# A lightning-attention kernel: second value weights loaded two units sooner, splits in halves, token normalisation on ScalarE, and other orders in the plain units and the first tile

## The chip, the cores and the metric

The kernel runs on one core of one Trainium2 chip. The metric is the device time in microseconds (us), the median of three runs. A core has five engines that work side by side, each with its own queue of instructions in order: TensorE (PE; its weight loads are listed as PEld) multiplies matrices into the accumulator memory PSUM, VectorE (DVE), ScalarE (ACT) and GpSimd (POOL) do elementwise work, and SyncE (SP) issues the transfers (DMAs) between the chip's main memory and the on-chip memory SBUF. ACT can issue DMAs too. An engine waits for another through semaphores; an instruction that waits holds up all that stand behind it in its queue.

## The reference

x has 4 sequences of 512 tokens with 512 features. Each token is normalised over its features (layer norm). Three things are computed from the normalised xn:

- q, k and v are silu of linear projections of xn, for 16 heads of 128. Within a sequence, blocks of tokens are taken in order, with a state that decays by a slope of the head:

```python
o_inter = einsum(qi * q_decay, kv)
o_intra = einsum(einsum(qi, ki) * diag_decay, vi)
kv_new  = block_decay * kv + einsum(ki * k_decay, vi)
```

- the heads' outputs are divided by their root mean square over all 2048 values, weighted, multiplied by sigmoid of another projection of xn (the gate), and projected back to 512 features: s.
- a router takes a softmax over 64 logits of xn, keeps the 8 largest weights, and forms xn times their sum plus a mix of 64 bias rows; silu of that is g.

The output is x + s * g. All inputs are 32-bit floats.

## The kernel before

**Products.** Each large product runs in a 32-bit matmul type on operands split in two: hi is the rounded value (`split_hi`, L99, always on ACT) and lo the rest (`split_lo`, L102, a subtraction on DVE or POOL). Three of the four hi/lo combinations are multiplied. Each projection is taken as a 2x2 by 2x2 block product. `unit` (L469) does it with seven products in place of eight (`PRODUCTS`, L39): the weights give A11, A12, A22 and four sums S1 to S4 (`sum_of`, L409), the tokens give B11, B21, B22 and four combinations T1 to T4 (`token_sums`, L261). A product is six matmuls of 128x512. Partial results are added on DVE from PSUM (L478), so a unit needs three PSUM banks, of four that there are. `plain_unit` (L510) does the eight plain products with A11, A12, A21, A22 and needs no sums.

**v's stage.** It comes first and is the one that the change touches. The 16 heads' v weights come in two halves, `ws[0]` and `ws[1]`; the tokens in two pairs of sequences p and four tiles t of 128 tokens a sequence. With `k` counting units, units 0 to 7 take all eight tile pairs with the first half, units 8 to 15 with the second (L900). Units 0 and 1 are plain ones, since the sums S are not ready then. A unit's silu is a sigmoid on ACT (`silu_of`, L536) and a product on DVE that is deferred (`do_deferred`) to a later point of the order.

**Tokens.** For each tile pair, `prepare` (L796) gives a list of steps: "stats" (`layer_norms`: mean and variance on DVE, and the reciprocal root on POOL by a power, L233), "norms" (`normalise_x`: one DVE operation a sequence, L205), "turn" (transposes on PE and copies to SBUF on ACT, and a store of the result), "sums" and "more" (combinations and splits of the token blocks, on POOL from the second tile on) and "logits" (router matmuls, L308). Unit k hosts the turn, sums, more and logits of tile k + 1, and stats and norms of tile k + 2, and issues the loads of tile k + 3.

**Order.** It is written out by hand. `after[i]` holds the steps that are issued after product i of a unit (`unit`), or after a pair of products in a plain unit (L526). All engines' queues follow this program order. Buffers are pools with a fixed count: the raw v weights have one buffer, the split v weights eight (tag "w"), x tiles four.

**Weights.** The first half's loads are interleaved with the first x loads (L859 to L864), its splits are spread over the start and units 0 and 1. The second half's eight loads of 256 KB are issued in unit 4 (L923), its sums in units 4 to 7 (two on DVE, two on POOL), its splits from unit 6 to unit 8 (L929).

**Start.** Slopes, the router weight and bias and norm_w are loaded from ACT's queue. ACT computes the decay tables `mkdecay` (16 activations of 128x256, exp) in two lots, four before the first split and 12 after the second tile's stats. POOL masks them, and 16 stores write them to main memory. `warm_up` runs transposes with no use of the result.

The stages after v's (gate, q and k projections and attention by heads, then the output projection) are the same in both kernels.

Of the kernel before, what the change touches and what calls it, by code (L numbers as in the profile page):

```python
# [50 lines left out]
def kernel(  # L51
# [13 lines left out]
    nc = tc.nc  # L65
# [5 lines left out]
    NT = N // P  # L71
# [18 lines left out]
    small = pool(ctx, "small", 4)  # L90
# [8 lines left out]
    def split_hi(hi, src):  # L99
        nc.scalar.copy(hi, src)  # L100
# [5 lines left out]
    slopes = const.tile([P, NH], F32, tag="slopes", name="slopes")  # L106
# [97 lines left out]
    def normalise(dst, src, b, t):  # L204
        nc.vector.tensor_scalar(  # L205
            dst, src, stats[b][:, t, 0:1], rstd[b][:, t : t + 1], ALU.subtract, ALU.mult
        )
# [8 lines left out]
    xts = {}  # L216
# [3 lines left out]
        nc.sync.dma_start(out=xt, in_=x[tok(b, t), :])  # L220
        xts[b, t] = xt

    def layer_norms(p, t):
        var = small.tile([P, PB], F32, tag="lnvar", name=f"lnv_{p}_{t}")
        for j in range(PB):
            b = p * PB + j
            st = small.tile([P, nc.vector.BN_STATS_DIM], F32, tag="bn", name=f"bn_{b}_{t}")
            nc.vector.bn_stats(st, xts[b, t])
            nc.vector.bn_aggr(stats[b][:, t, :], st)
            nc.vector.tensor_scalar(  # L230
                var[:, j : j + 1], stats[b][:, t, 1:2], 1.0, LN_EPS, ALU.mult, ALU.add
            )
        nc.gpsimd.tensor_tensor(rstd_of[p][:, t], var, mhalf[:, 0:PB], ALU.pow)  # L233

    def normalise_x(bs, t):
        for b in bs:
            normalise(xts[b, t], xts[b, t], b, t)

    xfs = {}

# [149 lines left out]
    class Weights:  # L390
# [37 lines left out]
        def place(self, n):  # L428
            self.of[n] = self.wp.tile([P, 2, self.width], F32R, tag="w", name=f"w_{n}_{self.name}")

        def split_one(self, n, eng):
            src = self.sum[int(n[1]) - 1] if n[0] == "S" else self.raw[:, int(n[1]) - 1, int(n[2]) - 1]
            if n not in self.of:
                self.place(n)
            split_hi(self.of[n][:, 0], src)

            m = 2 if eng is nc.gpsimd else 1
            for i in range(m):
                c = bass.ts(i, self.width // m)
                split_lo(eng, self.of[n][:, 1, c], src[:, c], self.of[n][:, 0, c])  # L440

        def splits(self, lo_engines):
# [67 lines left out]
    def plain_unit(name, operands, sink, after):  # L510
        for i in range(2):
            ps = [ps_mm.tile([P, N], F32, tag="mm", name=f"d{i}{j}_{name}") for j in range(2)]
            for k in range(2):
                for j in range(2):
                    xn = (("B11", "T1"), ("B21", "B22"))[k][j]
                    for c in range(KC):
                        for n, (wi, xi) in enumerate(PASSES):
                            lhsT, rhs = operands(f"A{i + 1}{k + 1}", xn, wi, xi, c)
                            nc.tensor.matmul(
                                ps[j], lhsT, rhs, start=(k == 0 and c == 0 and n == 0),  # L520
                                stop=(k == 1 and c == KC - 1 and n == len(PASSES) - 1),
                            )
                    if k == 1:
                        do_deferred()
                        sink(i, j, ps[j])
                for fs in after[3 * i + k :][: 1 if k == 0 else 2 + i]:  # L526
                    for f in fs:
                        f()

# [16 lines left out]
    def do_deferred(keep=0):  # L546
        while len(deferred) > keep:
            deferred.pop(0)()
# [245 lines left out]
    NP_FIRST = 2  # L794

    def prepare(stage, p, t):  # L796
        bs = [p * PB + j for j in range(PB)]

        def turn():
            for j in range(PB):  # L800
                transpose(stage, p, j, t)
            if p == 0:
                nc.sync.dma_start(out=xf_d[t], in_=xfs[p, t])

        if p == 0 and t < NP_FIRST:
            sums = (lambda: plain(p, t, nc.vector if t == 0 else nc.gpsimd)), lambda: None
        else:
            sums = combine(stage, p, t, nc.gpsimd)

        def route_logits():  # L810
            logits(stage, p, t)
        return {
            "stats": lambda: layer_norms(p, t), "norms": lambda: normalise_x(bs, t),
            "turn": turn, "sums": sums[0], "more": sums[1], "logits": route_logits,
        }

# [36 lines left out]
    ws = [v_weights(0, g, rawp, sump, vwp) for g in range(NV)]  # L853
# [2 lines left out]
    n1 = len(tiles)  # L856
    prep = [prepare(stage, p, t) for p, t in tiles]

    nc.scalar.dma_start(out=slopes, in_=slope.to_broadcast([P, NH]))  # L859
    load_pair(stage, 0, 0)  # L860
    vloads = ws[0].load()
    vloads(4)
    load_pair(stage, 0, 1)
    vloads(4)  # L864
    nc.scalar.dma_start(out=rw, in_=router_w)
    nc.scalar.dma_start(out=rb, in_=router_b.to_broadcast([P, E]))
    nc.scalar.dma_start(out=nw, in_=norm_w)
    make_first()
    make_dist()
    warm_up(WARM)  # L870
    for i, n in enumerate(XN):
# [8 lines left out]
    ds[0] = make_decays(ds[0], hs[0])  # L880
    prep[0]["stats"]()
    prep[0]["norms"]()
    ws[0].split_one("A11", nc.vector)
    prep[0]["turn"]()
    load_pair(stage, *tiles[2])
    mask_decays(ds[0], hs[0])
    warm_up(6)
    prep[0]["sums"]()
    ws[0].split_one("A12", nc.gpsimd)
    prep[0]["logits"]()  # L890
    prep[1]["stats"]()
    prep[1]["norms"]()
# [7 lines left out]
    for k, (p, t) in enumerate(tiles + again):  # L900
        g, after = k // n1, nothing()
        for unit_of, what in ((n1 - 3, (0, "top")), (n1 - 2, (0, "less")), (n1 + 2, (1, "top")), (n1 + 3, (1, "less"))):
            if k == unit_of:
                after[2].append(lambda what=what: scores_less(*what))
        if n1 - NT <= k < n1:
            after[6].append(lambda p=p, t=t: keep_blocks(p, t))
        if k + 1 < n1:
            after[0].append(prep[k + 1]["turn"])
            if k + 3 < n1:
                after[0].append(lambda k=k: load_pair(stage, *tiles[k + 3]))  # L910
            if k + 2 < n1:
                after[1].append(prep[k + 2]["stats"])
                after[2].append(prep[k + 2]["norms"])
            after[1].append(prep[k + 1]["sums"])
            after[4].append(prep[k + 1]["more"])
            after[4].append(prep[k + 1]["logits"])
        if k < NP_FIRST:
            for i in range(2 * k, 2 * k + 2):
                after[2 + 2 * (i % 2)].append(lambda i=i: ws[0].sum_of(i, nc.vector))
            for i, n in enumerate((("S1", "S2"), ("S3", "S4"))[k]):  # L920
                eng = nc.gpsimd if i else nc.vector
                after[2 * i + 3].append(lambda n=n, eng=eng: ws[0].split_one(n, eng))
        if k == n1 // 2:  # L923
            ws[1].load()()
        if n1 - 4 <= k < n1:
            n = k - n1 + 4
            eng = nc.gpsimd if n > 1 else nc.vector
            after[0 if n == 3 else 5 if n == 2 else 3].append(lambda n=n, eng=eng: ws[1].sum_of(n, eng))
        for n, unit_of, step, eng in (  # L929
            ("A11", n1 - 2, 6, nc.gpsimd), ("S2", n1 - 1, 0, nc.vector), ("S1", n1 - 1, 1, nc.gpsimd),  # L930
            ("A12", n1 - 1, 3, nc.vector), ("S3", n1 - 1, 4, nc.gpsimd), ("S4", n1, 0, nc.vector),
            ("A22", n1, 2, nc.vector),
        ):
            if k == unit_of:
                after[step].append(lambda n=n, eng=eng: ws[1].split_one(n, eng))
        if n1 <= k < n1 + NT:
            after[0].append(lambda t=t: load_xf(stage, t))
        if n1 < k <= n1 + NT:
            first, more = combine(stage, 0, k - n1 - 1, nc.gpsimd, "r")
            after[1].append(first)  # L940
            after[4].append(more)
        if k == n1 + NT + 1:
            after[1].append(scores_exp)
        if k == 2 * n1 - 1:
            vs_stack.close()
            todo = [(p, *u) for p in range(NP) for u in h_units(p, hw_stack)]
            todo[0][3].load()()
# [187 lines left out]
```

## Time and profile before

| what | value |
|---|---|
| median of three runs | 1090.64 us (1090.46 to 1091.09) |
| profiled execution, its own time | 1089.88 us |
| span of its instructions | 1088.2 us |
| mean granted TensorE clock | 0.995 |
| busy: PE, DVE, ACT, POOL | 98%, 63%, 44%, 66% |

The profile is of one execution. Times inside it count from the first instruction. A row of the timeline gives the start, the length, the engine, the line of the kernel, the operation with the tile that it writes and those that it reads (output before the arrow), the count of merged instructions, and, in brackets, how long the engine had been idle before and what ended that. A list of waits gives the total, the number and the longest. A row by stretch gives the stretch and its length, then for PE, PEld, DVE, ACT and POOL the busy time and the number of instructions, then the granted clock, the DMA share and the rate in GB/s. Matmuls overlap, so the time of a group of matmuls is best read from start to start.

### The profile page before, as it was taken

How to read it: one execution, taken by the hardware profiler on the slowest of the kernel's cores; microseconds unless marked ns; L12 is line 12 of the kernel's file. 1: busy time of each engine (PE TensorE's matmuls, PEld its weight loads, DVE VectorE, ACT ScalarE, POOL GpSimd, SP SyncE). 2: the span in 40 equal slices, each digit the busy share in tenths (PEclk: the TensorE clock that was granted, in tenths of full speed). 3: DMA queues.
4: the chain of work that ended last, by engine and by line, in shares of the span. 5: the costliest groups of instructions: out<-in, count | busy, mean ns of one | idle time of the engine just before them, and what ended most of it. 6: DMA issues, size and time to landing. Idle time of an engine off the chain costs nothing.

```text
span 1088.2 us, 16459 instructions
## 1 busy us (share of the span) xinstructions
PE 1063.4 (98%) x5762; PEld 912.5 (84%) x5762; DVE 686.9 (63%) x1052; ACT 480.1 (44%) x936; POOL 723.0 (66%) x725
## 2 busy tenths in 40 slices
PE   8898899999999999999999999999999999999998
PEld 7687788888888888888888888888888888788886
DVE  5687876667776755656646556556566574854554
ACT  6444545444444444444444444444444444322311
POOL 5686976586776786787777767877777656722130
PEclk9999999999999999999999999999999999999999
DMA  6546753433224222324742233222322427354351
GB/s 218 180 167 221 249 202 145 160 95 113 93 92 136 92 83 92 94 87 159 251 152 83 83 103 105 85 75 94 104 83 83 125 80 270 107 184 158 123 175 58
DMA packets 105059, 143.09 MB, mean 131 GB/s; under 512 B 9104, under 2 KB 53264, under 8 KB 104080
## 3 DMA queue, kind: packets, MB, share of 16 engines
q1 hardware_dynamic: 104112, 141.33, 39.4%
q8 instruction: 46, 0.75, 0.3%
q10 hardware_dynamic: 864, 0.70, 0.2%
q14 instruction: 37, 0.30, 0.1%
HBM read 91.14 MB, written 50.86 MB: 130 GB/s over the span
## 4 chain that ended last, share of the span: by engine, by line
PE 87%; DVE 5%; ACT 2%; issue 2%; POOL 1%; DMA 1%; SPq 1%; DVEq 0%; ACTq 0%; POOLq 0%
PE u_qk L487 27%; PE po L786 16%; PE u_g L487 14%; PE u_v L487 9%; PE sa L654 5%; PE o L691 5%; PE ss L677 4%; PE o L693 4%; PE kt L657 2%; DMA raw_v<-in_w_v_dram 1%; DVE vo_v L541 1%; PE pu L746 1%; PE lg L308 0%; DVE vo_v L478 0%; ACT w_A_v L100 0%
## 5 line engine op out<-in xcount | busy, mean ns | idle before, releaser
L786 PE MATMUL po<-wr,yr 128*128 128x512 f32 x768 | 179.9, 392 | 1.5 <-DVE u L780 1.5
L786 PEld LDWEIGHTS po<-wr,yr 128*128 128x128 f32 x768 | 144.9, 189 | 31.9 <-ACT yr L100 1.9
L487 PE MATMUL u_qk<-blk_T,ws_qk 128*128 128x512 f32 x576 | 149.1, 399 | 0.0
L703 POOL TENSOR_TENSOR sqs<-sqs,sq 128x512 f32<-128x512 f32 x60 | 77.8, 1297 | 89.5 <-ACT sq L702 85.9
L487 PEld LDWEIGHTS u_qk<-blk_T,ws_qk 128*128 128x128 f32 x576 | 104.7, 188 | 20.3
L681 DVE SCALAR_TENSOR_TENSOR st<-st,bdecay,ss 128x128 f32<-128x128 f32 x128 | 44.4, 347 | 105.3 <-ACT st L679 103.0
L487 PE MATMUL u_qk<-blk_B,wa_qk 128*128 128x512 f32 x384 | 99.5, 394 | 0.0
L103 DVE TENSOR_TENSOR yr<-yin,yr 128x512 fp32r<-128x512 f32 x64 | 68.0, 1097 | 46.9 <-ACT yr L100 45.7
L103 POOL TENSOR_TENSOR ws_qk<-sum_qk,ws_qk 128x512 fp32r<-128x512 f32 x64 | 88.5, 1398 | 13.3 <-ACT ws_qk L100 13.3
L691 PE MATMUL o<-at,vin 128*128 128x128 f32 x512 | 88.2, 274 | 0.0
L487 PEld LDWEIGHTS u_qk<-blk_B,wa_qk 128*128 128x128 f32 x384 | 70.9, 188 | 14.2
L691 PEld LDWEIGHTS o<-at,vin 128*128 128x128 f32 x512 | 77.2, 191 | 5.0
L487 PE MATMUL u_g<-blk_T,ws_g 128*128 128x512 f32 x288 | 78.1, 406 | 0.0
L663 ACT ACTIVATE kd<-kt,kdecay 128x384 f32<-128x384 f32 x64 | 37.3, 582 | 87.7 <-PE kt L657 87.7
L693 PE MATMUL o<-qd,st 128*128 128x128 f32 x384 | 74.2, 275 | 0.0
L654 PEld LDWEIGHTS sa<-q,k 128*128 128x128 f32 x512 | 66.5, 191 | 8.0 <-DVE q L541 2.7
L695 DVE SCALAR_TENSOR_TENSOR y<-o,nw,gt 128x512 f32<-128x512 f32 x64 | 47.8, 747 | 39.5 <-PE o L693 38.8
L538 ACT ACTIVATE sg_k<-k 128x512 f32<-128x512 f32 x64 | 40.5, 632 | 65.8 <-DVE k L478 65.8
L654 PE MATMUL sa<-q,k 128*128 128x128 f32 x512 | 67.8, 275 | 1.7 <-DVE q L541 1.6
L750 POOL TENSOR_TENSOR u<-u,sgu 128x512 f32<-128x512 f32 x16 | 20.7, 1295 | 73.0 <-ACT sgu L749 59.1
L487 PE MATMUL u_v<-w_S_v,blk_T 128*128 128x512 f32 x252 | 62.8, 393 | 3.7 <-DVE a_v L478 2.3
L665 POOL TENSOR_TENSOR qd<-q,dec 128x384 f32<-128x384 f32 x64 | 65.6, 1026 | 0.0
(182 smaller groups left out, 2429.9 us busy)
## 6 DMA issues: line engine op xcount, KB each, us to landing
v<-vo_v SPq DMA_DIRECT2D x64, 256.0 KB, 2.0
raw_qk<-in_w_head_dram SPq DMA_DIRECT2D x64, 256.0 KB, 4.0
vin<-v SPq DMA_DIRECT2D x64, 256.0 KB, 3.4
y<-y SPq DMA_DIRECT2D x64, 256.0 KB, 2.1
yin<-y SPq DMA_DIRECT2D x64, 256.0 KB, 3.8
x<-in_x_dram SPq DMA_DIRECT2D x32, 256.0 KB, 4.9
raw_g<-in_w_head_dram SPq DMA_DIRECT2D x32, 256.0 KB, 3.1
raw_v<-in_w_v_dram SPq DMA_DIRECT2D x16, 256.0 KB, 4.7
```

The source lines that it names most:

```text
L103: eng.tensor_tensor(lo, src, hi.bitcast(F32), ALU.subtract)
L487: nc.tensor.matmul(ps, lhsT, rhs, start=(first and c == 0 and n == 0), stop=(c == KC - 1 and n == len(PASSES) - 1), skip_group_check=not f ...
L538: nc.scalar.activation(sg, src, AF.Sigmoid)
L654: nc.tensor.matmul(pa[:, c], k[:, c], q[:, c], start=True, stop=True)
L665: nc.gpsimd.tensor_tensor(qd[s], q[:, 1:], d[:, 1, None, :].to_broadcast([P, NT - 1, P]), ALU.mult)
L677: nc.tensor.matmul(ps[:, c], kd[s][:, c], v_of(b, h, c), start=True, stop=True)
L681: nc.vector.scalar_tensor_tensor(r[:, c], r[:, c - 1], bdecay[:, h : h + 1], ps[:, c], ALU.mult, ALU.add)
L691: nc.tensor.matmul(o, v_of(b, h, c), at[s][:, c], start=True, stop=(c == 0))
L693: nc.tensor.matmul(o, st[s][:, c - 1], qd[s][:, c - 1], start=False, stop=True)
L695: nc.vector.scalar_tensor_tensor(y, po, nw[:, h : h + 1], gts[s], ALU.mult, ALU.mult)
L703: nc.gpsimd.tensor_tensor(sq[b], sq[b], s1, ALU.add)
L786: nc.tensor.matmul(pos[t], yr[:, yi, bass.ts(t, P)], wos[h][:, wi], start=(h == 0 and n == 0), stop=(h == NH - 1 and n == len(PASSES) - 1),)
```

## The change

- The second half's v weights are loaded in unit 2 in place of unit 4, and its four sums are formed in units 3 to 6, all on DVE, in place of 4 to 7 on DVE and POOL.
- The second half's splits: S2 and S4 go from DVE to POOL, S4 from unit 8 to the end of unit 7; A12 and A22 stay on DVE but come as two halves at two steps.
- `split_one` does the lo part always in two halves, for DVE too. It can do one piece alone, and with `hi` splits the hi part as well. Of the first half's weights, A11 has its hi part in halves, and A12's lo part goes half to POOL and half to DVE.
- The tokens of all tile pairs but the first are normalised by ACT (scale and bias as pointers) from a small `shift` that DVE computes; the first pair stays on DVE. For the first pair, POOL makes the reciprocal root of each sequence apart.
- In plain units, the deferred products are done at the head of each half's second point (before: only inside the second pair of products), and the steps are split 1, 2, 2, 2 over the four points (before 1, 2, 1, 3). Unit 0 turns the second tile after the second pair of products in place of the first.
- At the start, ACT does a small exp first (with the load of its function table), and then issues the four small loads; the constants are made by POOL before that in program order.

```diff
-    def layer_norms(p, t):
+    def layer_norms(p, t, apart=False):
...
+            if apart:
+                nc.gpsimd.tensor_tensor(
+                    rstd_of[p][:, t, j : j + 1], var[:, j : j + 1], mhalf[:, 0:1], ALU.pow
+                )
+        if not apart:
+            nc.gpsimd.tensor_tensor(rstd_of[p][:, t], var, mhalf[:, 0:PB], ALU.pow)
+
+    def normalise_x(p, t, vector=False):
+        for b in range(p * PB, p * PB + PB):
+            if vector:
+                normalise(xts[b, t], xts[b, t], b, t)
+                continue
+            shift = small.tile([P, 1], F32, tag="shift", name=f"shift_{b}_{t}")
+            nc.vector.scalar_tensor_tensor(
+                shift, stats[b][:, t, 0:1], -1.0, rstd[b][:, t : t + 1], ALU.mult, ALU.mult
+            )
+            nc.scalar.activation(
+                xts[b, t], xts[b, t], AF.Identity, bias=shift, scale=rstd[b][:, t : t + 1]
+            )
...
-        def split_one(self, n, eng):
+        def split_one(self, n, eng, piece=None, hi=False):
...
-            split_hi(self.of[n][:, 0], src)
-            m = 2 if eng is nc.gpsimd else 1
-            for i in range(m):
-                c = bass.ts(i, self.width // m)
+            for i in (0, 1) if piece is None else (piece,):
+                c = bass.ts(i, self.width // 2)
+                if hi:
+                    split_hi(self.of[n][:, 0, c], src[:, c])
+                elif i == 0:
+                    split_hi(self.of[n][:, 0], src)
                 split_lo(eng, self.of[n][:, 1, c], src[:, c], self.of[n][:, 0, c])
...
-                for fs in after[3 * i + k :][: 1 if k == 0 else 2 + i]:
+                if k == 0:
+                    do_deferred()
+                for fs in (after[0:1], after[1:3], after[3:5], after[5:7])[2 * i + k]:
...
-    nc.scalar.dma_start(out=slopes, in_=slope.to_broadcast([P, NH]))
     load_pair(stage, 0, 0)
     vloads = ws[0].load()
     vloads(4)
     load_pair(stage, 0, 1)
     vloads(4)
+    make_first()
+
+    nc.scalar.activation(kdecay[:, 0:NT], mhalf, AF.Exp)
+    nc.scalar.dma_start(out=slopes, in_=slope.to_broadcast([P, NH]))
     nc.scalar.dma_start(out=rw, in_=router_w)
     nc.scalar.dma_start(out=rb, in_=router_b.to_broadcast([P, E]))
     nc.scalar.dma_start(out=nw, in_=norm_w)
-    make_first()
...
-    ws[0].split_one("A11", nc.vector)
+    ws[0].split_one("A11", nc.vector, hi=True)
...
-    ws[0].split_one("A12", nc.gpsimd)
+    ws[0].split_one("A12", nc.gpsimd, 0)
+    ws[0].split_one("A12", nc.vector, 1)
...
-            after[0].append(prep[k + 1]["turn"])
+            after[0 if k else 1].append(prep[k + 1]["turn"])
...
-        if k == n1 // 2:
-            ws[1].load()()
-        if n1 - 4 <= k < n1:
-            n = k - n1 + 4
-            eng = nc.gpsimd if n > 1 else nc.vector
-            after[0 if n == 3 else 5 if n == 2 else 3].append(lambda n=n, eng=eng: ws[1].sum_of(n, eng))
-        for n, unit_of, step, eng in (
-            ("A11", n1 - 2, 6, nc.gpsimd), ("S2", n1 - 1, 0, nc.vector), ("S1", n1 - 1, 1, nc.gpsimd),
-            ("A12", n1 - 1, 3, nc.vector), ("S3", n1 - 1, 4, nc.gpsimd), ("S4", n1, 0, nc.vector),
-            ("A22", n1, 2, nc.vector),
+        if k == NP_FIRST:
+            after[0].append(ws[1].load())
+        if n1 - 5 <= k < n1 - 1:
+            after[3].append(lambda n=k - n1 + 5: ws[1].sum_of(n, nc.vector))
+        for n, unit_of, step, eng, piece in (
+            ("A11", n1 - 2, 6, nc.gpsimd, None), ("S2", n1 - 1, 0, nc.gpsimd, None),
+            ("S1", n1 - 1, 1, nc.gpsimd, None), ("A12", n1 - 1, 2, nc.vector, 0),
+            ("S3", n1 - 1, 3, nc.gpsimd, None), ("A12", n1 - 1, 4, nc.vector, 1),
+            ("S4", n1 - 1, 6, nc.gpsimd, None), ("A22", n1, 2, nc.vector, 0), ("A22", n1, 3, nc.vector, 1),
         ):
             if k == unit_of:
-                after[step].append(lambda n=n, eng=eng: ws[1].split_one(n, eng))
+                after[step].append(lambda n=n, eng=eng, piece=piece: ws[1].split_one(n, eng, piece))
```

More of the change, by code (lines that the diff above doesn't have):

```diff
@@ L232, in layer_norms @@
             )
[L233 to L237, printed above, removed]
+            if apart:
[16 more added lines that the diff above has]
+            )
     xfs = {}
@@ L796, in prepare @@
     def prepare(stage, p, t):
-        bs = [p * PB + j for j in range(PB)]
+        first = (p, t) == (0, 0)
         def turn():
@@ L812, in prepare @@
         return {
-            "stats": lambda: layer_norms(p, t), "norms": lambda: normalise_x(bs, t),
+            "stats": lambda: layer_norms(p, t, first), "norms": lambda: normalise_x(p, t, first),
             "turn": turn, "sums": sums[0], "more": sums[1], "logits": route_logits,
```

## The prediction

> **What bounds the kernel now.** First the page's busy line, then the busy time by stretch, then the list of what PE waited for.
>
> ```profile
> PE 1063.4 (98%) x5762; PEld 912.5 (84%) x5762; DVE 686.9 (63%) x1052; ACT 480.1 (44%) x936; POOL 723.0 (66%) x725
> ```
>
> PE is busy for 1063.4 of 1088.2 us, so everything that an edit of order can save lies in the remaining 24.8 us and in matmuls that ran slow. The stretches (us and instruction counts of PE, PEld, DVE, ACT, POOL, then clock, DMA share, GB/s) say where:
>
> ```profile
> 30.00:37.00 7.00, 4.32 (x16) 3.62 (x17) 4.35 (x6) 3.46 (x6) 1.56 (x3) 0.76 0.68 225
> 82.00:93.00 11.00, 7.75 (x38) 6.28 (x38) 7.43 (x10) 3.71 (x9) 7.44 (x10) 0.84 0.53 191
> 99.00:105.00 6.00, 5.50 (x30) 4.43 (x30) 6.00 (x10) 2.49 (x7) 6.00 (x7) 1.00 0.29 106
> 116.00:137.00 21.00, 18.20 (x78) 14.01 (x77) 19.80 (x21) 11.44 (x16) 19.06 (x12) 1.00 0.74 258
> ```
>
> All are in v's stage, before 137 us; after that PE's listed waits are short (1.6 and 1.5 us at most in total). In the last two rows DVE and POOL are full while PE has gaps; in the first two the clock is down. PE's waits:
>
> ```profile
> PE u_v L487 <- DVE vo_v L478: 4.2, 3, 3.2
> PE pt L248 <- DVE x L205: 3.5, 2, 1.8
> PE d_v L519 <- DVE vo_v L541: 3.2, 1, 3.2
> PE u_v L487 <- DVE a_v L478: 2.3, 2, 1.4
> ```
>
> (total, times, longest). All are PE waiting for DVE. The timeline shows what DVE was at (start, length, engine):
>
> ```profile
> 83.02 1.64 PE L487 MATMUL u_v<-w_S_v,blk_B 128*128 128x512 f32 x6
> 85.70 1.55 DVE L426 TENSOR_TENSOR sum_v<-raw_v 128x1024 f32<-128x1024 f32 x1 [2.87 <-DMA raw_v<-in_w_v_dram]
> 87.90 2.93 PE L487 MATMUL u_v<-w_A_v,blk_T 128*128 128x512 f32 x6 [3.25 <-DVE vo_v L478]
> 90.63 1.63 PE L487 MATMUL u_v<-w_A_v,blk_B 128*128 128x512 f32 x6
> ```
>
> DVE stood 2.87 us on the second weights' DMA, and the PSUM add (L478) that frees PE's bank was queued behind that sum.
>
> **The unit of account.** A group of six matmuls goes start to start in 1.36 us (66.33 to 67.69, warm). I count each stall by starts, so that refill and slow clock are in it.
>
> **Second weights two units sooner (loads in unit 2 for unit 4, sums in units 3 to 6 for 4 to 7, all on DVE).** Before, starts at 83.02, 87.90, 90.63, 92.10 for three groups: 9.08 - 3 x 1.36 = 5.0 us lost. After, eight loads of 256 KB are issued behind unit 2's x loads, near 54 us; at the old rate (76.05 to 85.6 from first issue to landing) they land near 64, and the first sum comes near 70. The eight issues take 4 us of SP's queue; behind them wait only unit 2's v stores, from 59.7 us. So -5.0. The price is a DVE sum of 1.75 us (the row at 44.16, beside a busy POOL) in units that had none; room for it comes from the normalisation.
>
> **ScalarE normalises (seven tiles of two).** DVE loses two operations of 0.94 us (median; 0.54 when POOL is idle) and gains two 128x1 ones of about 0.15 (row of lnv). Unit by unit 1.8 - 0.35 = 1.5 us come free and the sum takes 1.75. In unit 5 the sum at 99.86 made the add late and PE's next start 102.27 in place of 100.13 + 1.36: 0.8, and 0.1 of refill after it: 0.9. After, stats' chain gives rstd at 98.1, shifts to 98.8 behind the row maximum, sum to 100.6, add to 101.2, before PE's need at 101.5. So -0.9, with 0.3 us of margin. ACT pays: the nearest row is a 128x256 activation with one pointer, 498 ns; with 256 more elements (0.6 for 512 from 0.42 for 256 in its casts) and a second pointer about 0.8, so 1.5 us a tile pair. The Trainium skill (ScalarE: Activation LUTs, Rules for kernel authors) speaks against it: multiply and add belong on VectorE. By DVE's best row that is 0.54 against 0.8, 0.5 us a pair lost; by the row that holds here (0.94) it is even, and ACT is 44% busy. On the path it matters once, in unit 0, below. In later units it delays the first sigmoid by some 2.5 us (97.26 to about 99.8) and behind it the blk_T casts; POOL reaches these only after its blk_B work (74.36 in unit 3, the casts then being done near 73.4). Hidden, with 1 us of margin.
>
> **Units 7 and 8, where the weights change (116 to 137).** Starts 116.02 to 136.08 hold 12 groups: 20.06 - 16.34 = 3.7 us lost, all to 2 us DVE operations ahead of a short add. After, S2 and S4 leave DVE, A12 and A22 come in halves, and POOL gives up two sums (7.0 us) for S2 and S4.
>
> ```profile
> 123.22 2.11 DVE L103 TENSOR_TENSOR w_A_v<-raw_v,w_A_v 128x1024 fp32r<-128x1024 f32 x1
> 135.24 1.22 DVE L103 TENSOR_TENSOR w_A_v<-raw_v,w_A_v 128x1024 fp32r<-128x1024 f32 x1
> ```
>
> The same operation takes 1.22 alone and 2.11 beside POOL. The Trainium skill (SBUF — State Buffer, Who interferes with whom) says a VectorE operation with two SBUF inputs and a GpSimd read exclude each other for a whole instruction, which speaks against halves: each could wait out a POOL half (1.28 alone, 1.75 here). By the rows a half costs 1.1; by the rule 0.6 + 1.28 = 1.9. With A12's cast done near 121.4, the half ends at 122.5 or 123.3; the add of product 4 is due at 123, needed by 124.5: no stall either way. POOL's five splits, 3.0 us each from 117.3, end with S4 at 132.3, just when PE asks; at 3.5 each 1.5 late. I take 0.3 of it: -3.4.
>
> **Start and the two plain units (0 to 64 us).** Removed: PE's waits of 1.79 (17.01, the second tile's transposes, now behind A12's products) and 3.23 (32.68, a bank freed late, now by products at the head of each half), the latter with 1.2 slow matmul time. Added: slopes' DMA goes out behind a table load (1.28) and a small activation, at 2.25 in place of 0.78. By its own row (4.5 to land) it is there at 6.8; by that of norm_w, issued at 2.19 behind two others, at 8.5. Its own is nearest: 6.8. From kdecay (6.63) to the end of four mkdecay was 2.0, so A11's casts start at 8.85 (8.82 before): even. The first tile's x comes 0.5 sooner, but ACT is at A11: nothing.
>
> What counts is ACT's order after that:
>
> ```profile
> 12.90 4.91 ACT L168 ACTIVATE mkdecay<-dist,slopes 128x256 f32<-128x256 f32 x12
> 17.70 1.99 ACT L100 CAST w_A_v<-raw_v 128x1024 fp32r<-128x1024 f32 x2
> ```
>
> Before, the 12 mkdecay filled ACT's wait; A21 was cast by 18.75, in time for PE at 20.8. After, the second tile's normalisation stands ahead. DVE: A12's half to 13.95, scores 14.2, stats 2.1 to 16.3; POOL's rstd 17.05; shifts 17.4; ACT 17.3 to 18.75; 12 mkdecay to 23.55; A21's cast to 24.55, A22's 25.5, table 26.8, two sigmoids 27.9, xf 28.9. PE: A11 from 12.35, A12 to 17.9, transposes to 19.3, then idle until 24.55: 5.25 us, a new stall, with 1.6 of slow clock (the row 87.90 to 92.10 lost 1.5). A21 to 28.85, logits 30.65, A22 33.35, unit 1's B11 and T1 to 36.1 (35.26 before: the two removed stalls pay back nearly all), and unit 2 at 46.85 (46.50). POOL runs late beside it: A22 28.1, masks 31.05, rstd 31.8, blocks 36; S2, which hangs on DVE's second sum (37.8) and ACT's cast (38.85), to 41.5; rstd 44.0 behind xf, sigmoid, product and stats; four subtractions to 47.9, first block 48.7 (47.2 before), first blk_T 51.6 (51.44 before, where it waited for a sigmoid that now comes later). Start stage +0.5; POOL alone could leave 1 more in unit 3. Bounds: -1.5 if slopes and contention are kind (DVE's sums 1.2, not 1.75), +4 with slopes at 8.5 and the POOL chain 2 behind.
>
> **Sum.** -5.0 - 0.9 - 3.4 + 0.5 = -8.8. Against the profiled execution, 1088.2 span in 1089.88 us: 1079.4 in 1081.1. The runs' median is 0.76 above that execution: 1081.8, forecast 1082.
>
> **Rivals.** (1) The start stage costs 3 to 6 instead of 0.5: the 5.25 us stall plus a POOL that never catches up. For it: POOL at 9.96 busy of 10 between 20 and 30 us; against: it waited 5.4 and 3.5 us after that. -9.3 + 4.5: 1086. (2) The sums leave waits: four units, each late as in unit 5 (0.9), take 2 to 4 of the gain: 1085. For it the margins of 0.3 to 0.7; against it the freed 1.5. (3) Slower. ACT becomes a link between rstd and POOL: the normalisation holds ACT's queue until POOL's rstd, and POOL's blk_T work waits for casts behind it. It has 1 us of margin; to end 2.2 slower, 11 us must come from the six units that have it, so casts near 3 us later than worked out in each: 1094. Against: ACT idles 2.4 to 2.9 us there. (4) It does not do what it says: the raw buffer is single, and if its loads waited for the first weights' last readers late in unit 2, sums would stall again: 1089 to 1092. Against: the last sum of the first weights ended at 50.8, before the loads' turn.
>
> **Chances.** Worked case 0.55 (its own range 1079 to 1084.5), rival 1 0.17, rival 2 0.13, rival 3 0.10, rival 4 0.05. Faster by over 0.2% (2.2 us, about what this kernel's measurement can tell) 0.85, within 0.05, slower 0.10. The range 1078.5 to 1088 leaves out rivals 3 and 4 and the tails.
>
> **What would show it.** Right: no PE wait over 1 us between 64 and 137, clock 1.00 from 82 to 93, and 116 to 137's work done in some 3 us less. PE idle about 5 us before A21's product, near 19 to 25 us, with a lowered clock after it; no wait at the second half of unit 1's first pair. x's DVE rows of L205 down to two, 14 new ACT rows of about 0.8. Wrong: unit 2 starting after 50, ACT waits for shift that PE shares, POOL splits of the second weights over 3.5 us a pair, or PE still waiting on L478 adds behind sums.

## The result and the profile after

The changed kernel takes 1093.19 us (median of 13 runs, 1092.10 to 1094.70); the kernel before, run beside it on the same chip, 1090.77 (13 runs, 1089.74 to 1092.27). The ratio is 1.0021, 95% interval 1.0012 to 1.0030: a little slower, not 8.6 us faster, as was forecast (1082 against 1090.64). The profiled execution took 1093.11 us, with a span of 1091.3 against 1088.2 before.

From the page of the changed kernel, the busy times:

```profile
PE 1068.6 (98%) x5762; PEld 913.4 (84%) x5762; DVE 681.9 (62%) x1059; ACT 489.6 (45%) x952; POOL 722.6 (66%) x725
```

PE is busy for 5.2 us more than before (1063.4), for the same 5762 matmuls. It did not get more to do; it did the same more slowly. What stood still is in the list of its waits (total, number, longest):

```profile
PE d_v L537 <- ACT w_A_v L100: 5.1, 1, 5.1
PE u_v L505 <- POOL blk_T L103: 2.9, 4, 1.0
PE u_v L505 <- POOL blk_B L103: 1.6, 1, 1.6
PE d_v L537 <- DVE vo_v L561: 1.6, 1, 1.6
...
PE u_v L505 <- DVE vo_v L496: 0.7, 1, 0.7
...
PE u_v L505 <- POOL w_S_v L103: 0.6, 1, 0.6
```

Before, the long waits ended with DVE. Now the longest ends with ACT, and six in v's stage with POOL. The same four stretches as before (us and counts of PE, PEld, DVE, ACT, POOL, then clock, DMA share, GB/s):

```profile
30.00:37.00 7.00, 5.38 (x25) 4.21 (x25) 4.92 (x5) 2.84 (x4) 4.11 (x8) 1.00 0.81 262
82.00:93.00 11.00, 10.36 (x58) 8.76 (x57) 9.01 (x18) 7.19 (x16) 9.29 (x10) 1.00 0.26 99
99.00:105.00 6.00, 6.00 (x34) 4.91 (x33) 5.50 (x9) 5.24 (x13) 6.00 (x7) 1.00 0.28 106
116.00:137.00 21.00, 19.69 (x85) 15.45 (x84) 18.68 (x24) 12.46 (x17) 17.34 (x12) 1.00 0.81 285
```

In the last three PE is busier (10.36 for 7.75 us, 6.00 for 5.50, 19.69 for 18.20), and in all four the clock is 1.00. (The first has more too, 5.38 for 4.32, but holds other work: here the stalls of the start lie outside it, at 24 and 36 us.) The gain is there, and then it is lost. To see where, the same matmul of both kernels is set side by side, and the difference of their starts is read at points of the order (after minus before, us; worked out from the starts in the two traces):

```
unit 3, first product          63.49   65.98   +2.5
unit 4, before sums' old stall 78.60   81.94   +3.3
unit 4, behind it              90.63   89.19   -1.4
unit 7, weights change        116.02  115.49   -0.5
late in unit 8                137.44  135.18   -2.3
end of span                  1088.2  1091.3    +3.1
```

At 137 us, where the change's last edit lies, the changed kernel leads by 2.3 us. After that both kernels issue the same instructions, and 5.4 us are lost, little by little. In the stage of heads, six matmuls go start to start in 1.36 us before (307.55 to 308.91, to 310.27):

```profile
307.55 1.53 PE L487 MATMUL u_qk<-blk_T,ws_qk 128*128 128x512 f32 x6
308.91 1.52 PE L487 MATMUL u_qk<-blk_B,ws_qk 128*128 128x512 f32 x6
310.27 1.52 PE L487 MATMUL u_qk<-blk_T,wb_qk 128*128 128x512 f32 x6
```

and in 1.39 and 1.40 after, with no wait and at a granted clock of 1.00:

```profile
306.18 1.56 PE L505 MATMUL u_qk<-blk_T,ws_qk 128*128 128x512 f32 x6
307.57 1.56 PE L505 MATMUL u_qk<-blk_B,ws_qk 128*128 128x512 f32 x6
308.97 1.55 PE L505 MATMUL u_qk<-blk_T,wb_qk 128*128 128x512 f32 x6
```

The reason lies in where the tiles stand in SBUF. `shift` is a new tag of the pool `small`; its four buffers take 32 bytes each, and 128 bytes in all move 125 tiles that stand behind that pool: v's weights, most token blocks, and the weights of heads 0 to 3 of the output projection. The pools on the other side, with the heads' weights, stay. So the operands of a matmul moved against each other. In v's stage both moved together, and the pace is 226.7 ns a matmul in both kernels between 140 and 200 us.

In the output projection the effect is bare, since the first four heads' tiles moved and the others did not. The addresses are those that the built kernel gives its tiles; the ns are means of the distance of neighbouring starts in the trace, taken by how the moving operand's address differs from that of the weights that load meanwhile:

```
before: difference a multiple of 256 bytes          747 matmuls  226.9 ns
after:  difference a multiple of 256 bytes          605 matmuls  226.9 ns
after:  128 bytes more than a multiple of 256       143 matmuls  232.9 ns
```

In the first of the four sequences both operands of these heads moved, so their difference stayed a multiple of 256: there the means are 228 to 229 ns after and 228 to 231 before. It is the distance between the two that counts, not the place of one.

### The profile page after: what moved, and what is told of

The parts are those of the page before. It is cut to its first block, busy times and chain, and to the rows that moved or that the text cites. A ratio compares the mean times of both kernels' runs of the same rounds, so it can differ in the third digit from the quotient of the medians.

```text
span 1091.3 us, 16504 instructions
## 1 busy us (share of the span) xinstructions
PE 1068.6 (98%) x5762; PEld 913.4 (84%) x5762; DVE 681.9 (62%) x1059; ACT 489.6 (45%) x952; POOL 722.6 (66%) x725
## 4 chain that ended last, share of the span: by engine, by line
PE 84%; POOL 6%; DVE 4%; issue 2%; ACT 2%; DMA 1%; SPq 0%; DVEq 0%; POOLq 0%; ACTq 0%
PE u_qk L505 27%; PE po L806 16%; PE u_g L505 14%; PE u_v L505 6%; PE sa L674 5%; PE o L711 5%; PE ss L697 4%; PE o L713 4%; PE kt L677 2%; POOL ts L278 1%; POOL blk_B L103 1%; POOL blk_T L103 1%; PE pu L766 1%; DVE vo_v L561 1%; DMA raw_v<-in_w_v_dram 1%
```

## The experiments

Each run is judged by its ratio to the kernel before, whose median was 1090.7 to 1091.7 us in the three sets. A gain in us is the ratio's distance from 1 times 1091. A trace is one execution, and in the start stage one execution differs from the next by about 1 us: the kernels "early loads alone" and "splits on top of it" below have the program of the kernel before up to unit 2, and begin that unit 1.0 us later and 0.2 sooner than it. Differences of that size there are not read.

### Placement: the shift tiles in another pool

The changed kernel, with `shift` taken from the pool of v's stage, so that no operand of the large products moves:

```diff
-            shift = small.tile([P, 1], F32, tag="shift", name=f"shift_{b}_{t}")
+            shift = stage.tile([P, 1], F32, tag="shift", name=f"shift_{b}_{t}")
```

> The changed kernel, with its 4-byte shift tiles taken from the stage's own pool on the other side of SBUF, so that the pool of small tiles, and with it every tile behind it (token blocks, output weights), sits where it sat before the change; nothing else is changed. Address theory: the four shift buffers (128 bytes) moved blocks and output weights against the operands that stay put, which costs some 5 ns a matmul from 137 us on; then the lag stays near -2.3 us from 137 us to the end, heads 0 to 3 of the output projection go at 227 ns a matmul and not 233, and the time is about 1088.3 (5 us less than the changed kernel). Rival (the drift after 137 us comes from order, queues or contention that the change left behind): time stays near 1093, 233 ns stays.

Measured: 1088.62 us, ratio 0.9972 (0.9963 to 0.9982), against 1.0021 for the changed kernel: 5.3 us from a line that changes no instruction's work. The rows in the output projection, changed kernel first (120 matmuls, heads 0 to 3 among them with 48), then this one:

```profile
978.84 27.68 PE L806 MATMUL po<-wr,yr 128*128 128x512 f32 x120
1006.35 0.63 PE L766 MATMUL pu<-ebs,wTin 128*128 128x512 f32 x2
```

```profile
975.13 27.36 PE L806 MATMUL po<-wr,yr 128*128 128x512 f32 x120
1002.33 0.62 PE L766 MATMUL pu<-ebs,wTin 128*128 128x512 f32 x2
```

27.51 us against 27.20 from start to start, 0.31 more: 6.5 ns for each of the 48. The heads' stage goes back to the old pace as well: between 200 and 560 us neighbouring starts of 128x512 matmuls lie 229.5 ns apart on average, against 229.4 in the kernel before and 232.5 in the changed one. After 137 us this kernel still loses 1.4 us of its lead in the trace (2.6 to 1.2), 1.1 of them in one wait of PE for a weight split on POOL, at 203 us, which the other two do not have.

### Placement: pads in the kernel before

The opposite way: the kernel before, with 4, 2 or 8 unused tiles of 32 bytes in `small`, each set once by POOL at the start.

```diff
     def make_first():
+        for i in range(4):
+            nc.gpsimd.memset(small.tile([P, 1], F32, tag="pad", name=f"pad_{i}", bufs=4), 0.0)
```

128 bytes:

> The kernel before, with four small tiles of 4 bytes (128 bytes in all) added to the pool of small tiles and set to zero once at the start; no other edit. Address theory: v's stage is as before (its two operands move together or stay), the later stages lose some 5 us: about 1096. Rival (order): four memsets of 0.1 us, 1090.8.

64 bytes:

> The kernel before with 64 bytes more in the small pool (two tiles set once), which move the token blocks, v's tiles and the first four heads' operands of the output projection by 64 bytes against the rest. In the changed kernel the output projection's matmuls take 226.9 ns where the moving operand's address and that of the next weights differ by a multiple of 256, and 232.9 where by 128 more. Theory 1 (only a multiple of 256 is quick): 1094 to 1097, heads 0 to 3 of the output projection at 230 or more. Theory 2 (some unit of 64 or less decides and only 128 collides): 1090 to 1091.5.

256 bytes:

> The kernel before with 256 bytes more in the small pool (eight tiles set once). Theory 1 (the remainder by 256 decides): 1090 to 1091.5, all heads of the output projection at 227. Theory 2 (the farther the move the slower, or any move): 1094 to 1097 as with 128 bytes.

Measured:

```
pad    time us   ratio (95%)               heads 0 to 3 of the last two sequences
128    1096.31   1.0046 (1.0034-1.0059)    233 ns
64     1093.89   1.0029 (1.0018-1.0039)    229 to 230 ns
256    1090.59   0.9995 (0.9986-1.0004)    227 ns
```

128 bytes cost 5.0 us, about as much as the changed kernel loses; 256 cost nothing. 64 lie between, a little below what the first theory gave. So not the move counts but its remainder by 256. With 64 the pace is not an even one: in the last two sequences single starts lie 226, 229 and 232 ns apart in turn, and in the second sequence, at the same remainder, these heads go at 233. Why is not known. That a multiple of 256 is quick and 128 more is slow is shown for the output projection. In the heads' stage other things slow single matmuls too: the kernel before has a mean of 229.4 ns there (200 to 560 us) where the output projection has 226.7 (from 960 us on), and why was not tried.

### The second weights' early loads alone

```diff
-        if k == n1 // 2:
-            ws[1].load()()
...
+        if k == NP_FIRST:
+            after[0].append(ws[1].load())
+        if n1 - 5 <= k < n1 - 1:
+            after[3].append(lambda n=k - n1 + 5: ws[1].sum_of(n, nc.vector))
```

> The kernel before with one part alone: the second weights' loads in unit 2 and their sums in units 3 to 6, all on VectorE. By the prediction's term the stall at 84.7 us with its slow clock goes (5.0) and unit 5 and 7 and 8 gain a little since POOL has no sums: 1085 to 1086. Rival (the sums on VectorE stretch POOL's subtractions beside them and the adds behind them, as normalisation is still on VectorE): some 0.6 to 0.9 us come back in each of four units, 1088.

Measured: 1085.80 us, ratio 0.9951 (0.9939 to 0.9964), 5.3 us faster. The stall at 87.90 is gone, and a small one of the kind that rival 2 named is left: DVE's add behind a sum.

```profile
86.85 1.66 PE L487 MATMUL u_v<-w_A_v,blk_T 128*128 128x512 f32 x6 [0.50 <-DVE vo_v L478]
```

In units 7 and 8 it gains as well, with their old splits:

```profile
116.00:137.00 21.00, 19.93 (x86) 15.59 (x85) 18.16 (x22) 11.63 (x17) 10.89 (x7) 1.00 0.84 291
```

POOL was full there (19.06 of 21); without its two sums it has half its time free, and from 128.09 us on it is idle: DVE's old split of S4 then takes 1.21 us for 2.31 before. From 116.02 to 137.44 of the kernel before this trace gains 1.8 us, so not all of the 5.3 us belongs to the loads' stall.

### The splits of units 7 and 8 on top of it

To the early loads, the change's list of splits (S2 and S4 on POOL, A12 and A22 in two pieces on DVE) is added.

```diff
-            ("A11", n1 - 2, 6, nc.gpsimd), ("S2", n1 - 1, 0, nc.vector), ("S1", n1 - 1, 1, nc.gpsimd),
...
+            ("A11", n1 - 2, 6, nc.gpsimd, None), ("S2", n1 - 1, 0, nc.gpsimd, None),
...
+            ("S4", n1 - 1, 6, nc.gpsimd, None), ("A22", n1, 2, nc.vector, 0), ("A22", n1, 3, nc.vector, 1),
```

> The kernel before with the second weights' early loads and sums, and the change's new list of splits for units 7 and 8 (S2 and S4 on POOL, A12 and A22 on DVE in two pieces); everything else as before. The early loads alone measured 1085.8, and their trace has only two waits of 0.62 and 0.44 left in units 7 and 8, since POOL was freed of two sums. Theory 1 (the early loads already give most of what the prediction put down to the splits): the splits add between -1.0 and +0.5, so 1084.8 to 1086.3, and the waits move from DVE's adds to POOL's w_S_v. Theory 2 (the prediction's: the splits are worth 3.4 by themselves): 1083 or less.

Measured: 1085.91 us, ratio 0.9953 (0.9940 to 0.9966): nothing added. With the sums out of the way the old splits were no longer a stall to be saved.

### ScalarE's normalisation alone

```diff
-    def normalise_x(bs, t):
-        for b in bs:
-            normalise(xts[b, t], xts[b, t], b, t)
+    def normalise_x(stage, p, t, vector=False):
...
+            shift = stage.tile([P, 1], F32, tag="shift", name=f"shift_{b}_{t}")
```

> The kernel before with ScalarE's normalisation of all tile pairs but the first, alone (shift tiles in the stage pool, so that no operand of the matmuls moves). Theory 1 (the normalisation itself makes the start worse, since ACT waits for rstd ahead of 12 mkdecay and of A21's cast): a stall of some 4 to 5 us before A21's product near 20 to 25 us, unit 2 some 2 to 3.5 us later, and 0.5 to 1 given back in units 3 to 6: 1092 to 1094. Theory 2 (the normalisation is even and the start's loss comes from the order of the plain units or from the table load): 1090 to 1091, no stall at A21.

Measured: 1094.06 us, ratio 1.0026 (1.0015 to 1.0038), 2.8 slower. The profiled execution took 1096.49, the longest of nine; where unit 3 begins it is 3.5 us behind the kernel before. Two waits of PE show it, first for x (1.79 before, for DVE), then a new one for A21:

```profile
17.27 1.36 PE L257 MATMUL pt<-ident,x 128*128 128x128 f32 x8 [2.18 <-ACT x L244]
18.39 2.99 PE L528 MATMUL d_v<-w_A_v,blk_B 128*128 128x512 f32 x12
23.70 0.73 PE L528 MATMUL d_v<-w_A_v,blk_B 128*128 128x512 f32 x2 [2.32 <-ACT w_A_v L100]
```

ACT's rows say why: it stands 3.50 us before the normalisation, with 12 mkdecay and A21's cast queued behind.

```profile
16.40 1.52 ACT L244 ACTIVATE x<-x,shift,rstd 128x512 f32<-128x512 f32 x2 [3.50 <-DVE shift L241]
17.83 4.89 ACT L168 ACTIVATE mkdecay<-dist,slopes 128x256 f32<-128x256 f32 x12
22.62 1.98 ACT L100 CAST w_A_v<-raw_v 128x1024 fp32r<-128x1024 f32 x2
```

### ACT's order at the start

Both are the changed kernel with `shift` in the other pool (1088.62). In the first the 12 mkdecay stand behind the casts of A21 and A22:

```diff
-    for i in range(1, 4):
-        ds[i] = make_decays(ds[i], hs[i])
     ws[0].split_one("A21", nc.vector)
     ws[0].split_one("A22", nc.gpsimd)
+    for i in range(1, 4):
+        ds[i] = make_decays(ds[i], hs[i])
```

> As the changed kernel with its shift tiles in the stage's pool, and the 12 decay activations on ScalarE put behind the casts of A21 and A22 instead of ahead of them. If ScalarE's order made the start's loss: PE's wait of 5.1 us before A21 and the slow clock after it (1.5) go, and most of it stays won: 3 to 5 us under the run with the shift tiles moved alone, about 1084. If the chain over POOL (masks, reciprocal root, blocks) sets the start anyway, the stall only moves: within 1 us of that run, 1088.

Measured: 1088.25 us, ratio 0.9971 (0.9961 to 0.9982): no gain. The stall of 5.1 us moved to the router's matmuls, for xf, which ACT copies behind the mkdecay:

```profile
PE lg L323 <- ACT xf L264: 5.9, 2, 5.3
```

In the second they stand ahead of the second tile's normalisation:

```diff
-    prep[1]["norms"]()
     for i in range(1, 4):
         ds[i] = make_decays(ds[i], hs[i])
+    prep[1]["norms"]()
```

> The changed kernel with shift in the stage pool (measured 1088.6), and with the 12 mkdecay issued ahead of the second tile's normalisation on ACT, in the time in which ACT waited 3.95 us for shift. Theory 1 (ACT's order alone makes the start's loss): A21's cast by 21.3, PE at A21 near 20.5 to 21, no stall, unit 2 starts near 46.5, 2 to 3.5 us sooner: 1085 to 1086.5. Theory 2 (POOL, late since the start, binds units 2 and 3 whatever ACT does, as where the mkdecay went behind A22's cast): 1088 to 1088.6.

Measured: 1085.52 us, ratio 0.9942 (0.9930 to 0.9955), 3.3 less than with `shift` moved alone. Now ACT works through where it stood:

```profile
12.72 4.92 ACT L168 ACTIVATE mkdecay<-dist,slopes 128x256 f32<-128x256 f32 x12
17.53 1.51 ACT L250 ACTIVATE x<-x,shift,rstd 128x512 f32<-128x512 f32 x2
```

PE begins A21 at 20.03, having waited 0.28. The loss was ACT's idle time with work behind it (3.95 us before its normalisation at 16.75 in the changed kernel), not the work.

### The order of the plain units

Early loads and sums, and the change's order in units 0 and 1; DVE normalises.

```diff
-                for fs in after[3 * i + k :][: 1 if k == 0 else 2 + i]:
+                if k == 0:
+                    do_deferred()
+                for fs in (after[0:1], after[1:3], after[3:5], after[5:7])[2 * i + k]:
...
-            after[0].append(prep[k + 1]["turn"])
+            after[0 if k else 1].append(prep[k + 1]["turn"])
```

> The kernel before with the early loads and sums (alone 1085.8) and the change's order in the plain units: deferred products at the head of each half's second point, steps split 1, 2, 2, 2, the second tile turned after the second pair of products in unit 0. DVE normalises as before. Theory 1 (the two waits of 1.8 at 17 and 3.2 at 32.7 go for good, as the prediction had it for the start): 2 to 4 us faster than the early loads alone, 1082 to 1084. Theory 2 (DVE and POOL take it back by unit 3, as they do in the changed kernel): 1085.3 to 1086.3.

Measured: 1083.65 us, ratio 0.9929 (0.9915 to 0.9943), 7.7 us faster than before: the fastest, with the next one close behind. It is 2.8 us ahead of the kernel before where unit 2 begins and 2.2 where unit 3 does. But the wait for a bank was not removed, only shortened (3.23 before):

```profile
31.36 1.62 PE L519 MATMUL d_v<-w_A_v,blk_T 128*128 128x512 f32 x6 [2.66 <-DVE vo_v L543]
```

The extra call stands after the first pair of products of each half, at the head of the half's first point and not, as the list of the change has it, of its second. So the product that frees a half's second bank still stands on DVE behind the steps of the half's second point, here the third tile's normalisation and a sum. In the next kernel the deferred products are done after each pair of products, ahead of its steps (`do_deferred()` without the `if k == 0`).

> Early loads and sums and the new order of the plain units (together measured 1083.65), with the deferred products done after every pair of products of a plain unit, ahead of the steps that stand there. In the trace of that kernel PE waits 2.66 us before 31.36 for a bank; the product that frees it stands at 30.54 on DVE, behind the third tile's normalisation (3.50 at 25.98) and a sum (29.41), though its sigmoid was there by 22. Theory 1 (the place in DVE's queue is all): that wait goes, 1081 to 1082.5. Theory 2 (POOL, which PE waits for by 1.1 and 1.5 in unit 2, takes it back): 1083.3 to 1084.

Measured: 1083.89 us, ratio 0.9941 (0.9928 to 0.9955): no gain. PE comes to that point at 28.54, without the wait, and 17 us later waits 1.94 longer for POOL (it waited 1.11 there):

```profile
45.77 1.42 PE L487 MATMUL u_v<-w_A_v,blk_B 128*128 128x512 f32 x5 [3.05 <-POOL blk_B L103]
```

The rest went to a wait of 1.22 at 34.92 for DVE. POOL sets the end of the start stage, as the second theory and rival 1 of the prediction had it.

### ScalarE's normalisation where nothing else is at stake

The same, with ScalarE normalising only from the fourth tile pair on.

```diff
-        bs = [p * PB + j for j in range(PB)]
+        first = p * NT + t < 3
```

> The same, with ScalarE normalising the tile pairs from the fourth on (shift in the stage pool), so in units 1 to 5 but not in the start. Theory 1 (the prediction's: DVE is relieved, the four waits of up to 0.5 on its adds beside the early sums go, ACT hides the work): 0.8 to 2 us faster than without it. Theory 2 (what DVE gives up returns as waits for POOL's blk_T, three times 0.6 in the changed kernel): within 0.7 of it, or slower.

Measured: 1086.45 us, ratio 0.9959 (0.9946 to 0.9971), 2.0 slower than without it. DVE's four waits of up to 0.5 shrink to one of 0.4, but POOL's blk_T and one DVE add take their place between 60 and 137 us:

```profile
PE u_v L496 <- POOL blk_T L103: 1.9, 3, 0.6
PE u_v L496 <- DVE a_v L487: 1.6, 1, 1.6
PE u_v L496 <- DVE vo_v L487: 0.4, 1, 0.4
```

Unit 3 shows why nothing is won. With DVE normalising, POOL's rows from rstd to the start of blk_T:

```profile
66.37 0.70 POOL L233 TENSOR_TENSOR rstd<-lnv,mhalf 128x2 f32<-128x2 f32 x1 [1.94 <-DVE lnv L230]
...
69.48 1.71 POOL L263 TENSOR_TENSOR ts<-xf,ts 128x256 f32<-128x256 f32 x1
...
73.75 3.78 POOL L103 TENSOR_TENSOR blk_T<-ts,blk_T 128x256 fp32r<-128x256 f32 x4
```

With ACT normalising, POOL's and then DVE's sum:

```profile
67.00 0.70 POOL L233 TENSOR_TENSOR rstd<-lnv,mhalf 128x2 f32<-128x2 f32 x1 [2.37 <-DVE lnv L230]
...
68.48 1.74 POOL L272 TENSOR_TENSOR ts<-xf,ts 128x256 f32<-128x256 f32 x1
...
74.64 3.26 POOL L103 TENSOR_TENSOR blk_T<-ts,blk_T 128x256 fp32r<-128x256 f32 x4
...
68.41 1.21 DVE L435 TENSOR_TENSOR sum_v<-raw_v 128x1024 f32<-128x1024 f32 x1
```

From rstd to blk_T it is 7.38 us in the one and 7.64 in the other, against 6.34 in the kernel before (68.02 to 74.36), which has no sum there. The sum costs POOL 1.0 to 1.3 us wherever it falls. With DVE normalising, PE waits about 0.5 in each of units 3 to 5 for the add behind the sum; with ACT, 0.6 in each of units 4 to 6 for blk_T, and a shorter queue on DVE wins nothing. In units 3 to 6 the two traces swing within 1.2 us of each other. They end 2.4 apart: 0.6 come in unit 2, which one execution cannot tell from chance, 0.6 in units 3 to 6, 0.9 in units 7 and 8, where DVE's add is waited for 1.6 in place of 0.6, and 0.3 after that.

The sum ends at 69.62, and POOL's subtraction, begun beside it, 0.60 later at 70.22, nearly as if it had begun only then (0.74 alone). So the Trainium skill's rule (SBUF — State Buffer, Who interferes with whom), that such a pair excludes each other for a whole instruction, fits these rows.

## Why the prediction was wrong

The forecast's sum was 8.8 us faster; by the medians it came out 2.4 slower, and by the two traces 3.1. Of the 11.9 us between the forecast and the traces, 5.4 are the matmuls' pace after 137 us and 6.5 lie in v's stage, by the differences at the points above.

**The step that failed most: no term for the pace after 137 us.** The prediction wrote "after that PE's listed waits are short" and took the rest of the kernel as unchanged, since its instructions are. It looked at what the new tile costs DVE and ACT, not at where it stands. Its four 32-byte buffers raised the mean in the heads' stage from 229.4 to 232.5 ns (200 to 560 us), from 229.1 to 230.7 behind that (560 to 960), and cost 6 ns on a fifth of the output projection's matmuls. With some 970, 1110 and 143 matmuls in these groups that is 3.0 + 1.8 + 0.9 us, near the 5.4. This was none of the rivals, and the third rival's mechanism for a slower kernel (ACT as a link in units 2 to 7) did not occur: between 64 and 116 us PE waits for POOL, not for ACT, and POOL works from its rstd to blk_T with pauses of 0.1 us at most.

**Start and plain units: +0.5 forecast, +2.5 measured.** The stall at A21 was forecast as 5.25 us idle until 24.55 and came as this, from the changed kernel's timeline:

```profile
24.05 2.93 PE L537 MATMUL d_v<-w_A_v,blk_B 128*128 128x512 f32 x6 [5.06 <-ACT w_A_v L100]
26.77 1.80 PE L537 MATMUL d_v<-w_A_v,blk_T 128*128 128x512 f32 x6
28.41 1.90 PE L323 MATMUL lg<-rw,xf 128*128 128x64 f32 x16
...
36.08 1.63 PE L537 MATMUL d_v<-w_A_v,blk_T 128*128 128x512 f32 x6 [1.62 <-DVE vo_v L561]
...
50.43 1.43 PE L505 MATMUL u_v<-w_A_v,blk_B 128*128 128x512 f32 x5 [1.64 <-POOL blk_B L103]
```

The slow clock after it took 1.6 us, as worked out (24.05 to 28.41 for two groups of 1.36). What failed is "the two removed stalls pay back nearly all": the second was only shortened (1.62 for 3.23). At 36.08 PE waits again for a bank, since the freeing product stands on DVE behind the third tile's shifts (31.36 to 34.20, the second of them late) and a sum: the "products at the head of each half" did not bring it ahead of these, as the kernel with the plain units' order shows. And POOL's chain was 1.6 late in unit 2. The bounds held: -1.5 to +4. One step was wrong in the other direction: slopes does not go out behind the table load. Its DMA was issued at 0.93, while the load ran from 0.78 to 2.06, and kdecay began at 5.24 rather than 6.8; nothing came of it, since ACT then waited for other data.

**Loads early: -5.0 forecast, -4.8 measured** between the rows at 78.60 and 90.63. Right, with its mechanism: no stall and a clock of 1.00 from 82 to 93. That the experiment by itself measured -5.3 is in part luck: some 4.0 of its trace lie at this stall, 1.8 in units 7 and 8, and it pays some back in between.

**ScalarE's normalisation and unit 5: -0.9 forecast, +1.8 measured** from unit 3 to 116 us without the old stall. Unit 5 gained 0.8 (100.13 to 103.76 before, 99.54 to 102.36 after), but units 4, 5 and 6 have a wait for blk_T each (0.63 to 0.64), and these cost 0.9 each with refill. The step that failed is "Hidden, with 1 us of margin". It worked out when the casts for blk_T would be there; it was POOL that came late, beside the sums: from rstd to blk_T it took 7.60 us in unit 3 (70.48 to 78.08), 6.34 before. First the changed kernel, then the one before:

```profile
70.48 0.70 POOL L239 TENSOR_TENSOR rstd<-lnv,mhalf 128x2 f32<-128x2 f32 x1 [2.17 <-DVE lnv L231]
...
71.95 1.74 POOL L278 TENSOR_TENSOR ts<-xf,ts 128x256 f32<-128x256 f32 x1
...
78.08 3.27 POOL L103 TENSOR_TENSOR blk_T<-ts,blk_T 128x256 fp32r<-128x256 f32 x4
```

```profile
68.02 0.70 POOL L233 TENSOR_TENSOR rstd<-lnv,mhalf 128x2 f32<-128x2 f32 x1 [1.94 <-DVE lnv L230]
...
74.36 3.73 POOL L103 TENSOR_TENSOR blk_T<-ts,blk_T 128x256 fp32r<-128x256 f32 x4
```

The prediction weighed the rule of exclusion for the half splits of unit 7 and the longer sum on DVE (1.75), but its sum puts what the sums cost POOL at nothing; it is 1.26 here. Rival 2 came near in size (four times 0.9; it came three times) but named the adds behind the sums, not POOL. The price on ACT was right (0.8 each; two take 1.52), and the Trainium skill's advice to keep multiply and add on VectorE (ScalarE: Activation LUTs, Rules for kernel authors) held, though not for the cost of one operation: this edit costs 2.8 us by itself, most of it in the start by ACT's order, and 2.0 where only later tiles have it.

**Units 7 and 8: -3.4 forecast, -1.7 measured.** The 12 groups that the prediction counts took 16.58 us (115.49 to 132.07) for 20.06 before: 3.5 less, as forecast. But 1.75 were lost on the next group, with PE's waits of 0.58 for S4 (before 133.94) and 0.74 for an add behind A22's halves (before 135.18). POOL's five splits were to end at 132.3, with 0.3 us set aside for lateness, and ended at 133.88. A half on DVE was put at 1.1 by the rows, 1.9 by the rule; A12's first took 1.08, A22's two 3.33 together:

```profile
121.78 1.08 DVE L103 TENSOR_TENSOR w_A_v<-raw_v,w_A_v 128x512 fp32r<-128x512 f32 x1 [1.33 <-ACT w_A_v L100]
...
121.01 12.87 POOL L103 TENSOR_TENSOR w_S_v<-sum_v,w_S_v 128x512 fp32r<-128x512 f32 x8
...
131.10 3.33 DVE L103 TENSOR_TENSOR w_A_v<-raw_v,w_A_v 128x512 fp32r<-128x512 f32 x2
```

The second is nearer to the rule than to the row. More important is the cause: the gain was put down to the splits (POOL's two sums were to pay for S2 and S4), but POOL's freedom from the sums gives it without them. The early loads alone have 19.93 us of PE in that stretch, the changed kernel 19.69, and the splits on top of them add nothing.

So of the change's parts, alone or by difference: early loads -5.3, plain units' order about -2.4 on top, new splits 0, ScalarE's normalisation +2 to +2.8, the new tile's place +5.3. These do not add up to the measured +2.4: they meet in the same queues, each has an interval of about 1.3 us either way, and some edits were not tried by themselves (the exp ahead of the small loads, the halves of A11 and A12 at the start, and the first pair's separate reciprocal roots). The kernel with the first two only is 7.7 us faster than the one before.

## What to carry to other kernels

When a change adds even a tiny tile to a pool, compare the addresses of the big matmul operands before and after, and put new small tiles where they move nothing. When PE's busy time grows with the same instruction count and its waits do not explain it, look at the distance between starts, stage by stage. And before an operation is moved to an idle engine, ask what that engine's queue will do while it waits for the operation's inputs, and whom the freed engine will now meet.

## What was not expected of the hardware

- A 128x512 matmul started every 226.9 ns where moving operand and weights lay a multiple of 256 bytes apart, every 232.9 ns with 128 bytes more; with 64 more every 229 to 230 in two sequences and every 233 in a third. Over the kernel pads of 128 bytes cost 5.0 us and pads of 64 cost 3.2, at a granted clock of 1.00 in the stages concerned.
- A DMA from ACT's queue was issued 0.15 us after the start of a 1.28 us table load on ACT, not behind it.
- Where a DVE sum of 1.21 us and POOL's subtractions of 0.74 to 0.79 meet, POOL needs 1.74 for one of them, and the sum up to 1.75 where it begins within one of POOL's.
